# Where the start of a graph kernel gets its small weights: from GpSimd's queue early, or from SyncE's queue behind the large inputs

## The chip, the cores and the metric

The kernel runs on one core of one Trainium2 chip. Times are device microseconds of one execution; the profile is of one profiled execution of the same kernel. The engines are TensorE (PE in the profile, with PEld for its weight loads), VectorE (DVE), ScalarE (ACT), GpSimd (POOL) and SyncE (SP), which only issues transfers here. Transfers can be issued by SyncE, ScalarE and GpSimd.

## The reference

Two layers over 16 batches of 1024 nodes with 64 features, each with a residual and a layer norm. Cut to what is computed:

```python
# layer 0
Q = einsum('bnc,oc->bno', x, Wq) + bq
K = einsum('bnc,oc->bno', x, Wk) + bk
V = einsum('bnc,oc->bno', x, Wv)
score = softmax(einsum('bnc,bmc->bnm', Q, K), axis=1)
score = einsum('bnm,mc->bnc', score, adj)
x = layernorm(x + einsum('bnm,bmc->bnc', score, V))
# layer 1: both supports are adj
x1 = adj @ x
x2 = 2 * adj @ x1 - x
x_cat = concat([x, x1, x2, x1, x2], axis=-1)
x = layernorm(x + x_cat @ weight + bias)
```

The kernel holds the batches in eight pairs, so that a pair has 128 features. It forms adj times x first (the "first product", into a tile U), by a scheme with seven quarter products (p1 to p7) in place of eight, for which VectorE forms sums of quarters of adj and of x. The scores need only one combined weight of Wq and Wk. Of layer 1's five weight blocks three combined ones are left, made on VectorE and stored in the tile `raw`, with Wv and the bias in its last two rows; all five have the mean over their outputs taken away.

## The kernel before

The loads, in the order of the program:

```python
still = const.tile([P, P], FP, ...); nc.vector.memset(still, 0.0)
ident = const.tile([P, P], FP, ...); make_identity(nc, ident)
wq, wk = pair_weight("wq"), pair_weight("wk")        # cleared 128x128 tiles
halves = [slice(j * C, (j + 1) * C) for j in range(2)]   # C = 64
for s in halves:
    nc.scalar.dma_start(wq[s, s], wqT)
    nc.gpsimd.dma_start(wk[s, s], wkT)
for s in halves:
    nc.scalar.dma_start(bkp[s], bk[:, None])
for k in range(0, K8, 4):                             # pair 0 in two halves
    nc.sync.dma_start(xs[:, 0, k : k + 4], x_in[:, 0, k : k + 4])
for p in range(1, NP):                                # pairs 1 to 7
    nc.sync.dma_start(xs[:, p], x_in[:, p])
for k in (4, 5, 6, 7, 0, 1, 2, 3):                    # adj
    nc.sync.dma_start(aT[:, k], a_in[:, k])
for s in halves:
    nc.gpsimd.dma_start(w1s[s], w1.rearrange("(s c) o -> c s o", c=C))
    nc.gpsimd.dma_start(raw[s, 3], wvT)
nc.gpsimd.dma_start(raw[:, 4], b1[None, :].to_broadcast([P, C]))
```

The first work of TensorE. Idle turns multiply a tile of zeros and keep TensorE busy while it would wait:

```python
def transposed(p):
    pt = ps_tile("pt")
    for k in range(K8):
        nc.tensor.transpose(pt[:, ts(k, P)], xs[:, p, k, :], ident)
    nc.scalar.activation(xT[:, p], pt, AF.Copy)

def score_weight():          # transposes Wq and Wk
    ...
def score_weight_2(pm):      # their product, and the product with bk
    ...
def project(p):              # GY[p] = combined weight times xT[p], on TensorE and VectorE
    ...

idle_turns(6)
transposed(0)
idle_turns(3)
transposed(1)
pm = score_weight()
idle_turns(2)
transposed(2)
score_weight_2(pm)
for p in range(NP):
    if p + 3 < NP:
        transposed(p + 3)
    project(p)
```

Then the preparation of the weights, twelve instructions of VectorE, and the first product:

```python
w24 = const.tile([P, C], FP, tag="w24", name="w24")
nc.vector.tensor_add(w24, w1s[:, 2], w1s[:, 4])
...                                                   # combine, then take the means away
wv = pair_weight("wv")
for j in range(2):
    s = slice(j * C, (j + 1) * C)
    nc.vector.tensor_copy(wv[s, s], raw[s, 3])
...
S = left_tiles()
for n in (1, 2, 4, 3):
    left_sum(S, n)                                    # sums of quarters of adj, VectorE
step, sums = product(S, xs, by_pair(U), acc_group=1)
sums(1)                                               # sum of quarters of x, VectorE
for p in range(NP):
    nc.vector.tensor_reduce(mu[:, p], rows_of(p), AX.X, ALU.add)
...
for name in ("p2", "p1", "p5"):
    step(name, 0)
    step(name, 1)
```

The attention loop follows, with the layer norm and layer 1's weights (`wv` and `raw` are first used there), and then two more products with adj.

Of the kernel before, what the change touches and what calls it, by code (L numbers as in the profile page):

```python
# [9 lines left out]
FP = mybir.dt.float32  # L10
AF = mybir.ActivationFunctionType
ALU = mybir.AluOpType
AX = mybir.AxisListType
# [5 lines left out]
def gnn_kernel(  # L19
# [13 lines left out]
    nc = tc.nc  # L33
    ctx.enter_context(tc.manual_schedule())
    N, B, C = out.shape
    P = 128
# [8 lines left out]
    const = ctx.enter_context(tc.tile_pool(name="const", bufs=1))  # L45
# [14 lines left out]
    def pair_weight(name):  # L60
        w = const.tile([P, P], FP, tag=name, name=name)
        nc.vector.memset(w, 0.0)
        return w
# [3 lines left out]
    ident = const.tile([P, P], FP, tag="ident", name="ident")  # L67
    make_identity(nc, ident)
    wq, wk = pair_weight("wq"), pair_weight("wk")
    bkp = const.tile([P, 1], FP, tag="bkp", name="bkp")  # L70
    raw = const.tile([P, 5, C], FP, tag="raw", name="raw")
    w1s = const.tile([P, 5, C], FP, tag="w1s", name="w1s")
    halves = [slice(j * C, (j + 1) * C) for j in range(2)]
    for s in halves:
        nc.scalar.dma_start(wq[s, s], wqT)
        nc.gpsimd.dma_start(wk[s, s], wkT)
    for s in halves:
        nc.scalar.dma_start(bkp[s], bk[:, None])
    for k in range(0, K8, 4):
        nc.sync.dma_start(xs[:, 0, k : k + 4], x_in[:, 0, k : k + 4])  # L80
    for p in range(1, NP):
        nc.sync.dma_start(xs[:, p], x_in[:, p])
    for k in (4, 5, 6, 7, 0, 1, 2, 3):
        nc.sync.dma_start(aT[:, k], a_in[:, k])
    for s in halves:
        nc.gpsimd.dma_start(w1s[s], w1.rearrange("(s c) o -> c s o", c=C))
        nc.gpsimd.dma_start(raw[s, 3], wvT)
    nc.gpsimd.dma_start(raw[:, 4], b1[None, :].to_broadcast([P, C]))

    expo = const.tile([P, G], FP, tag="expo", name="expo")  # L90
    nc.vector.memset(expo, -0.5)
# [12 lines left out]
# [6 lines that stand above are left out]
# [14 lines left out]
    def rows_of(p):  # L124
        return xs[:, p].rearrange("p k (b c) -> p (k b) c", b=2)
# [7 lines left out]
    def idle_turns(n):  # L133

        pt = pacc.tile([P, N], FP, tag="acc", name="idle")
        for _ in range(n):
            nc.tensor.matmul(pt[:, 0:P], still, still, start=True, stop=True)

    idle_turns(6)
    transposed(0)  # L140
    idle_turns(3)
    transposed(1)
    pm = score_weight()
    idle_turns(2)
# [2 lines left out]
    for p in range(NP):  # L147
# [6 lines left out]

    w24 = const.tile([P, C], FP, tag="w24", name="w24")
    nc.vector.tensor_add(w24, w1s[:, 2], w1s[:, 4])
    nc.vector.tensor_sub(raw[:, 0], w1s[:, 0], w24)
    nc.vector.tensor_add(raw[:, 0], raw[:, 0], ident[:, 0:C])  # L160
    nc.vector.tensor_add(raw[:, 0], raw[:, 0], ident[:, C:P])
    nc.vector.tensor_add(raw[:, 1], w1s[:, 1], w1s[:, 3])
    nc.vector.tensor_scalar(raw[:, 2], w24, 2.0, None, op0=ALU.mult)
    rsum = const.tile([P, 5], FP, tag="rsum", name="rsum")
    nc.vector.tensor_reduce(rsum, raw, AX.X, ALU.add)
    nc.vector.scalar_tensor_tensor(
        raw, rsum[:, :, None].to_broadcast([P, 5, C]), -1.0 / C, raw, op0=ALU.mult, op1=ALU.add
    )
    wv = pair_weight("wv")
    for j in range(2):  # L170
        s = slice(j * C, (j + 1) * C)
        nc.vector.tensor_copy(wv[s, s], raw[s, 3])

    def row_sums(sq, g=G):
        var = small.tile([P, g], FP, tag="var", name="var")
# [45 lines left out]
    def by_pair(t):  # L221

        return t.rearrange("p k (q f) -> p q k f", q=NP)
# [189 lines left out]
        left_sum(S, n)  # L413
    step, sums = product(S, xs, by_pair(U), acc_group=1)
    sums(1)
    for p in range(NP):
        nc.vector.tensor_reduce(mu[:, p], rows_of(p), AX.X, ALU.add)
    nc.vector.tensor_scalar(mu, mu, 1.0 / C, None, op0=ALU.mult)
# [179 lines left out]
```

## Time and profile before

| what | value |
|---|---|
| time, median of 3 runs | 620.51 us (619.64 to 621.8) |
| span of the profiled execution | 619.1 us |
| VectorE, ScalarE, GpSimd busy | 54%, 36%, 13% of the span |
| transfers in all | 14.30 MB, 23 GB/s over the span |
| loads of x, adj at the start | 512 KB for each of 8 pairs of x, 8 of 512 KB for adj |

The span in 40 slices of 15.5 us shows TensorE and the transfers (a digit is the busy share in tenths; the first slice is the start that the change edits):

```profile
PE   7999999999999999999999999999999999999995
...
DMA  7700000200000000000000000000000000010012
```

The small transfers, from the page's list of issues (destination, source, issuing queue, count, KB of each, us from issue to landing):

```profile
w1s<-in_w_dram POOLq DMA_DIRECT2D x2, 80.0 KB, 9.1
wq<-in_wqT_dram ACTq DMA_DIRECT2D x2, 16.0 KB, 4.9
wk<-in_wkT_dram POOLq DMA_DIRECT2D x2, 16.0 KB, 6.0
```

A "wait" of an engine in the profile is idle time, put down to the event that ended it. The clock column of the stage views is the share of full speed that TensorE was granted.

### The profile page before, as it was taken

The numbers are of one execution on the slowest core, as the hardware profiler recorded it, in microseconds if no ns is written. First come the engines' busy times: TensorE is split into PE (matmuls) and PEld (weight loads), VectorE is DVE, ScalarE is ACT, GpSimd is POOL, SyncE is SP. The second block draws the span as 40 slices with busy tenths as digits, with TensorE's granted clock in tenths as the row PEclk, the third lists the DMA queues.
The fourth block names the chain that finished last, engine by engine and source line by source line (L and its number), as shares of the span: only waits on it lengthen the run. The fifth ranks groups of instructions, "written<-read, shape, count | busy, mean of one in ns | idle before, by whom it ended". The sixth has DMA issues, their size and how long they took to land. (4 is left out here: it accounts for less than half of the span.)

```text
span 619.1 us, 5817 instructions
## 1 busy us (share of the span) xinstructions
PE 606.8 (98%) x2268; PEld 265.7 (43%) x2268; DVE 337.2 (54%) x560; ACT 225.9 (36%) x379; POOL 82.7 (13%) x47
## 2 busy tenths in 40 slices
PE   7999999999999999999999999999999999999995
PEld 6544444433334344343434434344544444444442
DVE  0598202157786867768686776735462333224544
ACT  3210100056666667676666767651100000000011
POOL 3000004400030300303030020300000000150372
PEclk8999999999999999999999999999999999999999
DMA  7700000200000000000000000000000000010012
GB/s 267 295 0 1 0 1 0 69 0 0 2 1 0 2 0 2 1 0 2 1 0 2 0 2 1 0 1 0 1 0 0 1 0 0 1 68 0 34 69 102
DMA packets 5883, 14.30 MB, mean 23 GB/s; under 512 B 976, under 2 KB 1072, under 8 KB 5856
## 3 DMA queue, kind: packets, MB, share of 16 engines
q1 hardware_dynamic: 5280, 13.63, 5.9%
q8 instruction: 18, 0.29, 0.2%
q0 software_dynamic: 256, 0.26, 0.1%
q10 hardware_dynamic: 320, 0.03, 0.0%
q14 instruction: 9, 0.07, 0.0%
HBM read 9.73 MB, written 4.19 MB: 22 GB/s over the span
## 5 line engine op out<-in xcount | busy, mean ns | idle before, releaser
L327 DVE TENSOR_SCALAR_CACHE_REDUCE e<-sc 128x1024 f32<-128x1024 f32 x128 | 151.6, 1222 | 68.1 <-PE sc L320 68.1
L334 ACT ACTIVATE e<-e,nm 128x1024 f32<-128x1024 f32 x128 | 146.2, 1143 | 74.7 <-DVE e L327 74.6
L320 PE MATMUL sc<-xT,GY 64*128 64x512 f32 x512 | 128.1, 615 | 0.5 <-DVE e L327 0.5
L357 PE MATMUL acc<-e,us 128*64 128x512 f32 x512 | 124.0, 605 | 0.3 <-DVE us L345 0.3
L182 POOL TENSOR_TENSOR rstd<-var,expo 128x16 f32<-128x16 f32 x13 | 37.7, 2902 | 421.5 <-DVE var L177 421.5
L320 PEld LDWEIGHTS sc<-xT,GY 64*128 64x128 f32 x512 | 44.6, 186 | 73.5 <-issue 49.9
L521 ACT ACTIVATE sq<-GY 128x1024 f32<-128x1024 f32 (+1 forms) x10 | 8.9, 886 | 159.6 <-DVE GY L297 149.9
L281 PE MATMUL p<-T,S 128*128 128x512 f32 x144 | 62.8, 592 | 0.0
L357 PEld LDWEIGHTS acc<-e,us 128*64 128x64 f32 x512 | 31.0, 136 | 71.0 <-issue 62.9
L281 PEld LDWEIGHTS p<-T,S 128*128 128x128 f32 x144 | 27.4, 190 | 34.4 <-issue 34.4
L299 ACT ACTIVATE U<-p 128x1024 f32<-128x1024 f32 x6 | 6.1, 1023 | 76.3 <-PE p L281 76.3
L393 PEld LDWEIGHTS pw<-raw,xT 64*128 64x128 f32 x256 | 21.8, 187 | 17.3 <-issue 7.3
L440 POOL TENSOR_TENSOR xs<-xs,mu 128x1024 f32<-128x1024 f32 x8 | 15.0, 1902 | 100.9 <-DVE T L250 90.1
L393 PE MATMUL pw<-raw,xT 64*128 64x192 f32 x256 | 27.1, 332 | 0.0
L404 DVE TENSOR_TENSOR xT<-pw,raw 128x256 f32<-128x256 f32 x32 | 13.6, 425 | 21.3 <-ACT GY L403 21.3
L334 ACT ACTIVATION_READ_ACCUMULATOR e<-e,nm 128x1 f32 x128 | 24.0, 188 | 0.0
L109 ACT ACTIVATE xT<-pt 128x1024 f32<-128x1024 f32 x16 | 16.2, 1013 | 20.0 <-PE pt L108 20.0
L108 PE MATMUL pt<-ident,xs 128*128 128x128 f32 x128 | 18.7, 294 | 3.0 <-DMA xs<-in_x_dram 3.0
L281 PE MATMUL acc<-T,aT 128*128 128x512 f32 x48 | 21.4, 594 | 0.0
L281 PE MATMUL p<-GY,aT 128*128 128x512 f32 x48 | 21.3, 596 | 0.0
L281 PE MATMUL p<-T,aT 128*128 128x512 f32 x48 | 21.3, 592 | 0.0
L281 PE MATMUL acc<-T,S 128*128 128x512 f32 x48 | 21.1, 592 | 0.0
(120 smaller groups left out, 594.5 us busy)
## 6 DMA issues: line engine op xcount, KB each, us to landing
aT<-in_adjT_dram SPq DMA_DIRECT2D x8, 512.0 KB, 10.1
out_dram<-GY SPq DMA_DIRECT2D x16, 256.0 KB, 2.2
xs<-in_x_dram SPq DMA_DIRECT2D x7, 512.0 KB, 9.0
aT<-in_adjT_dram SPq DMA_DIRECT2D x1, 1024.0 KB, 5.0
xs<-in_x_dram SPq DMA_DIRECT2D x2, 256.0 KB, 3.0
w1s<-in_w_dram POOLq DMA_DIRECT2D x2, 80.0 KB, 9.1
wq<-in_wqT_dram ACTq DMA_DIRECT2D x2, 16.0 KB, 4.9
wk<-in_wkT_dram POOLq DMA_DIRECT2D x2, 16.0 KB, 6.0
```

Of the source, the lines that this page charges most:

```text
L108: nc.tensor.transpose(pt[:, ts(k, P)], xs[:, p, k, :], ident)
L109: nc.scalar.activation(xT[:, p], pt, AF.Copy)
L182: nc.gpsimd.tensor_tensor(rstd, var, expo[:, 0:g], ALU.pow)
L281: nc.tensor.matmul(pt[:, ts(i, H)], left_of(k, 2 * g + i), right_of(k), start=(start and k == 0), stop=(k == HB - 1), skip_group_check=not ...
L320: nc.tensor.matmul(sc[j][:, ts(h, H)], GY[s, p, ts(m, P)], xT[s, p, ts(h, H)], start=True, stop=True,)
L327: nc.vector.tensor_scalar(E[n][:, j], sc[j], -1.0, None, op0=ALU.mult, op1=ALU.min, accum_out=NM[n][:, j : j + 1],)
L334: nc.scalar.activation(E[n][:, j], E[n][:, j], AF.Exp, bias=NM[n][:, j : j + 1], scale=-1.0, accum_out=SM[n][:, j : j + 1],)
L357: nc.tensor.matmul(ACC[p][j * C : (j + 1) * C, ts(h, H)], us[:, j], es[:, j, ts(h, H)], start=(m == 0), stop=(m == K8 - 1),)
L393: nc.tensor.matmul(pw[:, j, ts(k, 3 * C)], xT[s, p, ts(2 * c + k, P)], raw[s, 0:3].rearrange("p w c -> p (w c)"), start=True, stop=True,)
L404: nc.vector.tensor_tensor(at(xT), to[:, 0], raw[:, 4:5, None].to_broadcast([P, 2, 2, C]), ALU.add)
L440: nc.gpsimd.tensor_tensor(rows_of(p), rows_of(p), mu[:, p, :, None].to_broadcast([P, G, C]), ALU.subtract)
L521: nc.scalar.activation(sq, r, AF.Square)
```

## The change

Seven transfers leave GpSimd's queue. Wk goes to SyncE's queue, behind the first pair of x and ahead of the second. The second layer's weights, Wv and the bias go to the end of SyncE's queue, behind adj. Since these land later, their preparation on VectorE moves behind the first sums of adj and x. One idle turn is added between the first two pairs. The aim is that the small transfers should not stand in the way of x at the start. No arithmetic changes.

```diff
     for s in halves:
         nc.scalar.dma_start(wq[s, s], wqT)
-        nc.gpsimd.dma_start(wk[s, s], wkT)
     for s in halves:
         nc.scalar.dma_start(bkp[s], bk[:, None])
     for k in range(0, K8, 4):
         nc.sync.dma_start(xs[:, 0, k : k + 4], x_in[:, 0, k : k + 4])
+    for s in halves:
+        nc.sync.dma_start(wk[s, s], wkT)
     for p in range(1, NP):
         nc.sync.dma_start(xs[:, p], x_in[:, p])
     for k in (4, 5, 6, 7, 0, 1, 2, 3):
         nc.sync.dma_start(aT[:, k], a_in[:, k])
     for s in halves:
-        nc.gpsimd.dma_start(w1s[s], w1.rearrange("(s c) o -> c s o", c=C))
-        nc.gpsimd.dma_start(raw[s, 3], wvT)
-    nc.gpsimd.dma_start(raw[:, 4], b1[None, :].to_broadcast([P, C]))
+        nc.sync.dma_start(w1s[s], w1.rearrange("(s c) o -> c s o", c=C))
+        nc.sync.dma_start(raw[s, 3], wvT)
+    nc.sync.dma_start(raw[:, 4], b1[None, :].to_broadcast([P, C]))
 ...
     idle_turns(6)
     transposed(0)
-    idle_turns(3)
+    idle_turns(4)
     transposed(1)
 ...
-    w24 = const.tile([P, C], FP, tag="w24", name="w24")
-    nc.vector.tensor_add(w24, w1s[:, 2], w1s[:, 4])
-    ...                                   (the twelve instructions, unchanged)
+    def layer_weights():
+        w24 = const.tile([P, C], FP, tag="w24", name="w24")
+        nc.vector.tensor_add(w24, w1s[:, 2], w1s[:, 4])
+        ...
+        return wv
 ...
     step, sums = product(S, xs, by_pair(U), acc_group=1)
     sums(1)
+    wv = layer_weights()
     for p in range(NP):
         nc.vector.tensor_reduce(mu[:, p], rows_of(p), AX.X, ALU.add)
```

More of the change, by code (lines that the diff above doesn't have):

```diff
@@ L150, in gnn_kernel @@
         project(p)
-    w24 = const.tile([P, C], FP, tag="w24", name="w24")
-    nc.vector.tensor_add(w24, w1s[:, 2], w1s[:, 4])
[L159 to L172, printed above, removed]
+    def layer_weights():
+        w24 = const.tile([P, C], FP, tag="w24", name="w24")
+        nc.vector.tensor_add(w24, w1s[:, 2], w1s[:, 4])
+        nc.vector.tensor_sub(raw[:, 0], w1s[:, 0], w24)
+        nc.vector.tensor_add(raw[:, 0], raw[:, 0], ident[:, 0:C])
+        nc.vector.tensor_add(raw[:, 0], raw[:, 0], ident[:, C:P])
+        nc.vector.tensor_add(raw[:, 1], w1s[:, 1], w1s[:, 3])
+        nc.vector.tensor_scalar(raw[:, 2], w24, 2.0, None, op0=ALU.mult)
+        rsum = const.tile([P, 5], FP, tag="rsum", name="rsum")
+        nc.vector.tensor_reduce(rsum, raw, AX.X, ALU.add)
+        nc.vector.scalar_tensor_tensor(
+            raw, rsum[:, :, None].to_broadcast([P, 5, C]), -1.0 / C, raw, op0=ALU.mult, op1=ALU.add
+        )
+        wv = pair_weight("wv")
+        for j in range(2):
+            s = slice(j * C, (j + 1) * C)
+            nc.vector.tensor_copy(wv[s, s], raw[s, 3])
+        return wv
     def row_sums(sq, g=G):
```

## The prediction

> **What bounds the kernel now.** I read the busy line of the page first, then stages cut at the places where TensorE (PE) changes its work, then PE's list of waits, then the start in order of time.
>
> The busy line and the stages (start:end, length, then busy time and instruction count of each engine, the granted PE clock, the DMA share and GB/s):
>
> ```profile
> PE 606.8 (98%) x2268; PEld 265.7 (43%) x2268; DVE 337.2 (54%) x560; ACT 225.9 (36%) x379; POOL 82.7 (13%) x47
> ...
> 1.05:6.25 5.20, 5.20 (x26) 4.99 (x26) 0.26 (x4) 1.92 (x2) 4.56 (x8) 1.00 0.74 239
> 6.25:9.28 3.03, 0.00 (x0) 0.00 (x1) 0.00 (x0) 0.39 (x1) 0.00 (x0) 0.91 0.64 222
> 9.28:12.25 2.97, 2.97 (x14) 2.97 (x15) 0.43 (x1) 0.96 (x1) 0.00 (x0) 0.52 1.02 316
> 12.25:31.20 18.95, 18.95 (x85) 11.35 (x84) 9.14 (x9) 6.20 (x7) 0.00 (x0) 1.00 0.78 309
> 31.20:100.00 68.80, 68.80 (x162) 30.52 (x161) 34.92 (x33) 6.14 (x6) 3.98 (x3) 1.00 0.00 0
> 100.00:406.00 306.00, 305.53 (x1442) 122.96 (x1440) 205.48 (x427) 188.25 (x325) 44.60 (x20) 1.00 0.01 4
> 406.00:598.00 192.00, 191.75 (x517) 87.19 (x514) 75.48 (x69) 17.26 (x31) 22.12 (x10) 1.00 0.03 11
> ```
>
> The reader is to see that PE sets the time. From 12.25 us to 598 us it is idle for 0.47 + 0.25 = 0.72 us in all, so whatever happens before 12.25 us shifts everything after it, one for one. Before that point lies one hole of 3.03 us with no PE work, and behind it 2.97 us of work at a clock of 0.52. Those two rows are all that this change can reach on PE. PE's waits, and the PE rows around the hole (start, duration, work, and in brackets the idle time before it and its cause):
>
> ```profile
> PE pt L108 <- DMA xs<-in_x_dram: 3.0, 1, 3.0
> PE idle L137 <- DVE still L66: 1.1, 1, 1.1
> PE sc L320 <- DVE e L327: 0.5, 1, 0.5
> PE acc L357 <- DVE us L345: 0.3, 1, 0.3
> ```
>
> ```profile
> 5.42 0.83 PE L137 MATMUL idle<-still 128*128 128x128 f32 x6
> 9.28 1.97 PE L108 MATMUL pt<-ident,xs 128*128 128x128 f32 x8 [3.03 <-DMA xs<-in_x_dram]
> ...
> 12.25 1.04 PE L108 MATMUL pt<-ident,xs 128*128 128x128 f32 x8
> ```
>
> The hole is the wait for the second pair of x, xs[1]. The same eight transposes take 1.97 us after it and 1.04 us one pair later.
>
> Why is xs[1] late? Its transfer is issued at 1.65 us and takes 7.6 us to land (the DMA view of that issue alone). Sizes and times to landing of undisturbed transfers stand on the page:
>
> ```profile
> xs<-in_x_dram SPq DMA_DIRECT2D x2, 256.0 KB, 3.0
> aT<-in_adjT_dram SPq DMA_DIRECT2D x1, 1024.0 KB, 5.0
> ```
>
> Between them lie 768 KB in 2.0 us, so 512 KB should land in about 3.7 us, half of what it took. In the hole the DMA engines are only 0.64 busy at 222 GB/s: the bandwidth is not used up, something in the mix is slow. The mix is xs on SyncE's queue, Wq and bk on ScalarE's, and seven transfers issued by GpSimd between 1.59 and 5.9 us (Wk twice, the weights twice, Wv twice, the bias). SyncE's own waits show one thing more:
>
> ```profile
> SPq L84 <- DMA xs<-in_x_dram: 3.9, 5, 0.9
> SPq L84 <- DMA bkp<-in_bk_dram: 1.9, 1, 1.9
> SPq L82 <- DMA xs<-in_x_dram: 1.0, 1, 1.0
> SPq L82 <- DMA wq<-in_wqT_dram: 0.5, 1, 0.5
> SPq L82 <- DMA bkp<-in_bk_dram: 0.4, 1, 0.4
> ```
>
> A load of x has no use for Wq or bk, yet it waits for them. After four SyncE and four ScalarE transfers, each further one waits for the landing of an older one. The ninth (xs[3]) was issued at 3.62 us, just when the first half of pair 0 had landed (issued at 0.74, 2.9 us to landing). I read this as eight completion places, shared by the two hardware queues.
>
> **What the Trainium skill says.** (1) "TensorE: Matmul & The Clock Gate", Part 1: The HAM clock gate: a PE idle for a window of about 3.4 us falls to half clock, for at least one window. This trace agrees: 0.52 in the stage behind the hole, and 1.00 from 12.25 us on. (2) "DMA: Bandwidth & Descriptors", Issuing engines are not separate DMA queues: transfers of all issuers share the same 16 engines and interleave, so Wk by SyncE saves no bandwidth; it can only change the order and the way descriptors are made. The trace agrees as far as it goes: during GpSimd's issues xs[1] takes twice its fitted time. (3) The same page, Latency and other measured facts: two of the sixteen DMA engines (7 and 15) are usually slower than the rest, as a best guess because the descriptor rings of GpSimd-issued transfers lie in SBUF behind their ports; transfers issued by SyncE or ScalarE have no such ring. No view here names the DMA engines; a transfer that ends late while the engines are 0.64 busy would fit.
>
> **The change part by part.**
>
> Removed from the start: all seven GpSimd transfers. They carry 2 x 16 + 2 x 80 + 2 x 16 + 32 = 256 KB, half the size of xs[1]. GpSimd's 4.3 us of issue go too, which nobody waited for.
>
> Added ahead of xs[1]: two Wk issues on SyncE, at about 0.45 to 0.6 us each (0.43 for an x issue; 0.6 estimated from ScalarE's two Wq issues in 1.19 us), and 32 KB in the queue, under 0.1 us at 370 GB/s, perhaps twice that since the rows have 256 bytes. SyncE would then be ready to issue xs[1] at about 2.6 to 2.8 us instead of 1.65. But the order is now four ScalarE transfers, pair 0 in two halves, Wk twice: eight. So xs[1] should be the ninth and wait for the first half of pair 0, at 3.64 us. With 3.7 us of flight it lands at about 7.3 us, 2.0 us sooner than the 9.28 of now.
>
> Idle turns, three to four: three turns are six records in 0.83 us, so the fourth costs 0.28 us. The turns then end at 6.25 + 0.28 = 6.53 us, still ahead of 7.3, so this costs nothing. The hole shrinks from 3.03 us to about 0.75 us.
>
> The clock: it was full until about 8.74 us (0.74 in the half microsecond from 8.5) and half for about 3.4 us then. In the 3.4 us before the drop PE worked 0.9 us. With the change it works about 1.2 us before the short hole and 1.4 us after it in the same stretch. I expect it to stay at 1.00. Then pair 1's work runs warm: eight transposes 1.04 us, two weight transposes at 0.13 each 0.27, two idle turns 4 x 0.138 = 0.55, together 1.86 instead of 2.97: 1.11 us less.
>
> Sum: the transposes of pair 2 start at 7.3 + 1.86 = 9.16 us, against 12.25: 3.1 us earlier.
>
> Does what follows keep up? xs[2] is issued when Wq's first half has landed (4.4 us now) and follows xs[1] in the queue by 512 KB at about 400 GB/s (the rate of 14 to 26 us), 1.3 us: 8.6 us, ahead of 9.16. xs[3] by 9.9, wanted at about 10.3. From there a pair costs PE 2.59 us (16.12 to 18.71 in the start's order of time), against 1.3 us for its transfer, so the queue gains. bk is wanted at about 10.3 us; now its second half lands at 3.0 + 9.3 = 12.3 us, in the same crowd that slows xs[1]; without the crowd I expect it by 9. This is the closest margin. adj has wide slack: first used at 31.2 now, landed by 28.6.
>
> Layer weights on VectorE: the twelve instructions run from 33.04 to 35.99 us, 2.95 us. They move behind the first five sums of 2.29 us each. The sums start 2.95 us sooner relative to PE, but PE waits for none of them now (after the very first clearing of a tile, the list has 0.8 us of VectorE waits, both in the attention loop), and the first product that needs one, p5, starts at 59.1. The reductions of x and the first add into U come behind the same total of VectorE work as before. Worth 0. The weights land behind adj, by about 27 us, and VectorE wants them at about 41 us: no wait. Five more SyncE issues end long before SyncE's next job.
>
> **The rivals.** (a) xs[1] lands as late as now, because the slow part is bk's four-byte rows on ScalarE's queue or the load itself: for it, SyncE also waits 1.9 us for bk; against it, that bk too is slowed in the same crowd. Then there is hardly a gain: 620 to 620.5. (b) The ninth place is not where I put it and xs[1] goes out at 2.7 us: landing at 6.4, no hole at all, pair 2 at 6.53 + 1.86 = 8.39, 3.9 us gained: 616.6. (c) The wait moves to bk or xs[3]: PE stops at 10.3 us for up to 2 us: 618 to 619.5. (d) The hole shrinks but the clock still drops: 1.1 us of the gain lost, about 618.5. (e) VectorE work becomes late for the products: would cost up to 3 us, but VectorE is 54% busy and the total ahead of each consumer is unchanged, so I give it little.
>
> **Range and chances.** 620.5 - 3.1 = 617.4. The three times before spread over 2.2 us, from 619.64 to 621.8. With about two thirds on (b) or the main line (616.6 to 617.8), a fifth on (c) and (d), the rest on (a), the range is 616.0 to 619.8. The whole stretch that can be won is 3.03 + 1.11 = 4.1 us, 0.7%, so 2% faster cannot be reached; 2% slower needs a wait of 12 us that nothing here shows.
>
> **What would show it.** Right: PE's wait for xs under 1 us; a clock of 1.00 from the first transposes on; pair 2's transposes at 8.4 to 9.5 us; xs[1] issued near 3.6 us with 3.5 to 4 us of flight; everything after 12.25 us the same, about 3 us earlier. Wrong: a new PE wait at the bk product or at a later pair; the clock at 0.5 somewhere in 8 to 13 us; xs[1] landing after 8 us; a VectorE wait on PE in the first product stage.

## The result, and the profile after

| | before | after |
|---|---|---|
| median of 6 runs | 621.32 us (619.64 to 623.32) | 617.92 us (617.77 to 618.05) |
| ratio | 1 | 0.9945, 95% interval 0.9926 to 0.9964 |
| span of the profiled execution | 619.1 us | 616.0 us |
| first matmul of the first product | 31.64 us | 28.93 us |

The change saves 3.4 us by the medians, 2.2 to 4.6 us by the interval; 617.92 lies in the predicted range. The changed kernel is also steadier: its six runs lie within 0.3 us, those of the kernel before within 3.7 us.

The stages of the kernel after, cut at the same places as in the prediction (start:end, length, busy time and count of PE, PEld, DVE, ACT, POOL, granted PE clock, DMA share, GB/s):

```profile
1.05:6.25 5.20, 5.20 (x28) 5.12 (x28) 0.26 (x4) 1.98 (x2) 0.25 (x1) 1.00 0.64 188
6.25:9.28 3.03, 1.50 (x14) 1.34 (x13) 0.00 (x0) 0.53 (x2) 0.00 (x0) 1.00 1.02 368
9.28:12.25 2.97, 2.97 (x26) 2.73 (x26) 0.78 (x3) 2.21 (x3) 0.00 (x0) 1.00 1.02 417
12.25:31.20 18.95, 18.95 (x70) 10.14 (x69) 11.05 (x9) 4.76 (x5) 0.00 (x0) 1.00 0.76 283
```

PE's waits and its start in order of time, after:

```profile
PE pt L109 <- DMA xs<-in_x_dram: 1.5, 1, 1.5
PE idle L138 <- DVE still L66: 1.1, 1, 1.1
PE sc L323 <- DVE e L330: 0.5, 1, 0.5
PE acc L360 <- DVE us L348: 0.3, 1, 0.3
```

```profile
5.36 1.06 PE L138 MATMUL idle<-still 128*128 128x128 f32 x8
7.95 1.10 PE L109 MATMUL pt<-ident,xs 128*128 128x128 f32 x8 [1.53 <-DMA xs<-in_x_dram]
...
9.54 1.04 PE L109 MATMUL pt<-ident,xs 128*128 128x128 f32 x8
...
10.78 1.07 PE L109 MATMUL pt<-ident,xs 128*128 128x128 f32 x8
...
28.93 11.32 PE L284 MATMUL p<-xs,aT 128*128 128x512 f32 x26
```

The reader is to see three things. The hole in front of pair 1 is 1.53 us instead of 3.03. The clock no longer falls: it is 1.00 from 6.25 us on. (The column has 1.00 in the first stage too, before and after, but the start of that stage is slow in both: the eight transposes of pair 0 take 1.80 us before and 1.75 us after, those of pair 2 1.04 us in both.) And between 6.25 and 9.28 us the transfers move 368 GB/s instead of 222. From pair 3's transposes (10.78 us, 13.49 before) on, PE's work is that of before, 2.71 us earlier: I compared the matmuls of each tile in the two traces at their first, middle and last, and the shift is 2.71 to 2.72 us up to the last one, 611 us into the span. The other 0.4 us between the two spans lie behind the last matmul, in the end of the output.

### The profile page after: what moved, and what is told of

Its sections match the earlier page's. It is cut to its first block, busy times and chain, and to the rows that moved or that the text cites. A ratio compares the mean times of both kernels' runs of the same rounds, so it can differ in the third digit from the quotient of the medians.

```text
span 616.0 us, 5816 instructions
## 1 busy us (share of the span) xinstructions
PE 605.6 (98%) x2270; PEld 264.4 (43%) x2270; DVE 337.1 (55%) x560; ACT 226.0 (37%) x379; POOL 78.4 (13%) x40
## 5 line engine op out<-in xcount | busy, mean ns | idle before, releaser
L284 PE MATMUL p<-S,aT 128*128 128x512 f32 x48 | 21.1, 592 | 0.0
```

Of the source, the lines that this page charges most:

```text
L284: nc.tensor.matmul(pt[:, ts(i, H)], left_of(k, 2 * g + i), right_of(k), start=(start and k == 0), stop=(k == HB - 1), skip_group_check=not ...
```

## The experiments

The figures of the start are from one profiled execution of each kernel, in us from the span's start, so some tenths between two rows may be chance: the four rows of the changed order (after, after_again, prep_first, three_turns) have xs[3] at 10.44 to 10.91. The medians come from several chips; the ratios further down compare with the kernel before on the same chip. "Lands" is the last of a transfer's completions in the trace. Up to sixteen DMA engines work on one transfer and each reports its share (the Trainium skill, "DMA: Bandwidth & Descriptors", Why a DMA increments its semaphore by 16 and not by 1; the traces have sixteen completions for each of these loads). The last column but one is the start of pair 3's transposes.

| kernel | xs[1] issued | xs[1] lands | xs[3] lands | pair 3 | median, us |
|---|---|---|---|---|---|
| before | 1.65 | 9.24 | 13.35 | 13.49 | 620.3 to 621.3 |
| wk_only | 3.49 | 7.84 | 13.09 | 13.23 | 620.70 |
| bridge | 1.66 | 6.66 | 12.62 | 12.76 | 620.31 |
| rest_late | 1.64 | 8.82 | 11.77 | 11.91 | 618.87 |
| rest_late_bk | 1.65 | 8.47 | 11.40 | 11.53 | 619.01 |
| after | 3.65 | 7.90 | 10.44 | 10.78 | 617.92 |
| after_again | 3.62 | 7.45 | 10.88 | 11.01 | 618.13 |
| prep_first | 3.53 | 7.88 | 10.48 | 10.76 | 618.08 |
| three_turns | 3.70 | 7.42 | 10.91 | 11.05 | 618.09 |
| wk_behind_x1 | 1.64 | 6.63 | 11.12 | 11.25 | 618.51 |
| x1_first | 1.63 | 6.31 | 10.83 | 10.96 | 618.08 |
| bk_behind_x2 | 2.84 | 6.91 | 11.51 | 11.64 | 618.98 |
| pair0_whole | 2.70 | 8.13 | 12.06 | 12.20 | 619.19 |
| x_first | 1.65 | 8.87 | 11.32 | 12.27 | 620.02 |

In all but three rows (after, prep_first and x_first) pair 3 starts 0.13 to 0.14 us after xs[3] has landed, and in all but x_first, which has another order of work, the first product starts 18.14 to 18.15 us after pair 3. xs[1] explains the product's start nowhere nearly so well: it lands between 6.3 and 9.2 us with little relation to it.

### Each half of the change alone

wk_only: Wk on SyncE behind pair 0; the other loads stay on GpSimd, the preparation stays in its old place, three turns.

```diff
     for s in halves:
         nc.scalar.dma_start(wq[s, s], wqT)
-        nc.gpsimd.dma_start(wk[s, s], wkT)
 ...
+    for s in halves:
+        nc.sync.dma_start(wk[s, s], wkT)
     for p in range(1, NP):
```

> The kernel before with Wk alone moved to SyncE behind pair 0; the layer-1 weights, Wv and the bias stay on GpSimd at the start, three idle turns. Theory (the crowd of GpSimd transfers slows xs[1], and the ninth transfer waits for pair 0's first half): xs[1] goes out near 3.65 us, meets the weights in flight, lands no earlier than 9 us, and nothing is gained: 620 to 622.5, a clock of 0.5 behind the hole. Rival (Wk's place is what brings the gain): xs[1] lands by 8 us and the time is 618 to 619.

Measured: ratio 1.000 (0.9989 to 1.001). The time is what the theory said, the reason is not: xs[1] landed at 7.84 us, as the rival had it. PE in order of time, wk_only:

```profile
7.88 1.10 PE L109 MATMUL pt<-ident,xs 128*128 128x128 f32 x8 [0.98 <-DMA xs<-in_x_dram]
...
11.92 1.06 PE L109 MATMUL pt<-ident,xs 128*128 128x128 f32 x8 [2.28 <-DMA xs<-in_x_dram]
```

The wait for pair 1 shrank and one of 2.28 us for pair 2 stood in its place; pair 3 then started 0.26 us sooner than before. So curing the hole that the profile of before shows is worth nothing by itself: xs[3] landed at 13.09 us, hardly sooner than the 13.35 of before.

rest_late: only the weights, Wv and the bias move behind adj; Wk stays on GpSimd, the preparation in place.

```diff
-        nc.gpsimd.dma_start(w1s[s], w1.rearrange("(s c) o -> c s o", c=C))
-        nc.gpsimd.dma_start(raw[s, 3], wvT)
-    nc.gpsimd.dma_start(raw[:, 4], b1[None, :].to_broadcast([P, C]))
+        nc.sync.dma_start(w1s[s], w1.rearrange("(s c) o -> c s o", c=C))
+        nc.sync.dma_start(raw[s, 3], wvT)
+    nc.sync.dma_start(raw[:, 4], b1[None, :].to_broadcast([P, C]))
```

> The kernel before with only the weights, Wv and the bias moved behind adj on SyncE; Wk stays on GpSimd, the preparation stays where it was, three idle turns. Theory: five GpSimd transfers fewer, and xs[1] still goes out at 1.65 us with no ninth place in its way, so it lands at 5.5 to 7.5 us, as early as or earlier than in the changed kernel (7.9 us); the clock stays at 1.00; 616.5 to 618. Rival (any GpSimd transfer in front slows it, or Wk's move was needed): xs[1] lands after 8.5 us, 619 to 621.

Measured: ratio 0.9978 (0.9967 to 0.9989). xs[1] landed at 8.82 us, hardly sooner than before, so the theory's landing (5.5 to 7.5) failed, and yet the first product came 1.59 us earlier, because xs[3] landed at 11.77 instead of 13.35. PE in order of time, rest_late:

```profile
8.87 1.10 PE L108 MATMUL pt<-ident,xs 128*128 128x128 f32 x8 [1.89 <-DMA xs<-in_x_dram]
...
11.91 1.06 PE L108 MATMUL pt<-ident,xs 128*128 128x128 f32 x8
```

The two halves together (0.27 and 1.59) are less than the whole (2.71 us). The medians on one chip say the same: 620.58 before, 620.70 wk_only, 618.87 rest_late, 618.08 with the changed order (prep_first).

What rest_late does not tell apart: its five transfers both leave GpSimd's queue and move their 224 KB behind x. No run issued them late from GpSimd, or early from SyncE. By an estimate from the traces (later pairs of x, 512 KB each, land 1.28 us apart) 224 KB take 0.56 us, so the bytes alone would not account for the 1.58 us by which xs[3] came sooner.

### The clock, the place of the preparation, the fourth turn

bridge: `idle_turns(3)` becomes `idle_turns(13)` in the kernel before.

> The kernel before with 13 idle turns instead of 3 between the first two pairs (ten more, 2.8 us), nothing else. Theory: xs[1] still lands at about 9.3 us, but PE works through the wait, the clock stays at 1.00, and only the slow part is won: pair 2 starts at about 11.1 instead of 12.25 us, 1.1 us less, 619.3 to 620.3. Rival (the clock falls by its own schedule and not by the hole): no gain.

Measured: ratio 0.9997 (0.9984 to 1.0009), no gain in the median to be told from noise: neither the theory's gain nor the rival's falling clock. Only the highest times are gone: its 12 runs reach at most 621.09 us, and 11 of the 43 runs of the kernel before beside it lie above that. In its profile the clock did hold, and pair 2 started at 10.78 us instead of 12.25. But xs[3] came at 12.62 us:

```profile
9.24 1.04 PE L108 MATMUL pt<-ident,xs 128*128 128x128 f32 x8
...
10.78 1.04 PE L108 MATMUL pt<-ident,xs 128*128 128x128 f32 x8
...
12.76 1.06 PE L108 MATMUL pt<-ident,xs 128*128 128x128 f32 x8 [0.59 <-DMA xs<-in_x_dram]
```

xs[1] here landed at 6.66 us, in the same order of loads as before: the order alone does not fix when it lands.

prep_first: `wv = layer_weights()` goes back in front of `S = left_tiles()` in the changed kernel.

> The changed kernel with the twelve instructions for the weights put back in front of the sums of adj. Theory (their place is worth 0, as PE never waits for VectorE there): 617.7 to 618.1, the same as the changed kernel, the first product at the same 28.9 us. Rival: the sums come late for the product p5 and PE waits up to 3 us: 619 to 621.

Measured: 618.08 us, ratio 0.9963 (0.9951 to 0.9976); the first product at 28.91 us. The place of the preparation is worth nothing that shows.

three_turns and after_again: the changed kernel with `idle_turns(3)`, and the changed kernel itself beside it.

> The changed kernel with three idle turns as before the change. Theory (the fourth turn lies in the wait for xs[1] and the clock holds without it): PE's wait for xs[1] 0.1 to 0.3 us longer, the first product at the same 28.9 us, 617.8 to 618.1 with the same narrow spread. Rival (the fourth turn is what keeps the clock up): some runs 1 us longer, median 618.3 to 619.

> The changed kernel once more, beside the other two on the same chip: 617.7 to 618.2, the first product at 28.7 to 29.1 us.

Measured: 618.09 us (617.52 to 618.35), ratio 0.9947 (0.9927 to 0.9967), and 618.13 us (617.78 to 619.14), ratio 0.9945 (0.992 to 0.9969). The fourth turn is worth nothing here. Both profiles had a second short wait, for xs[3] (0.61 and 0.48 us), and so the first product at 29.19 and 29.16 us, a little later than expected.

### Is it GpSimd's queue that slows xs[1], and can the start be shortened further?

Four kernels with Wk on SyncE or GpSimd, and bk on ScalarE or behind xs[2]. wk_behind_x1, x1_first and bk_behind_x2 start from the changed kernel, rest_late_bk from rest_late:

```diff
     for p in range(1, NP):
         nc.sync.dma_start(xs[:, p], x_in[:, p])
+        for s in halves:
+            if p == 1:                               # wk_behind_x1, x1_first
+                nc.sync.dma_start(wk[s, s], wkT)
+            elif p == 2:                             # x1_first, bk_behind_x2, rest_late_bk
+                nc.sync.dma_start(bkp[s], bk[:, None])
```

(each with the old load of the same tensor taken out)

> The changed kernel with Wk behind the second pair of x instead of ahead of it. xs[1] is then among the first eight transfers and goes out at 1.65 us, as in rest_late, and no GpSimd transfer is left. Theory A (GpSimd-issued transfers are what slows xs[1]): it lands 4.2 us later, near 6 us; PE's wait for it is gone, Wk lands by 8 us; the first product starts near 28 us, 616.8 to 617.5. Theory B (small rows on ScalarE's queue, Wq and bk, beside a large load slow it in the same way): it lands after 8 us as in rest_late (8.9), the first product at 29 us or later, 618 to 619.

> The same with bk also moved to SyncE, behind xs[2]: only Wq is on ScalarE's queue. Theory A: as wk_behind_x1, near 6 us, 616.8 to 617.5, unless bk now comes late for its product at 9.5 us. Theory B: xs[1] now lands by 6.5 us, about 2 us sooner than in wk_behind_x1, and the time is about 1 us lower than there.

> The changed kernel with bk moved to SyncE behind xs[2], Wk still ahead of xs[1]. xs[1] becomes the seventh transfer and goes out at 2.8 us instead of 3.65. Theory (the ninth place costs what it looks like): it lands about 0.8 us sooner, near 7.1 us, and the first product starts 0.8 us sooner, near 28.1: 617.0 to 617.4. Rival (the stop for the ninth place is what lets the small rows through; xs[1] then flies as much longer as it leaves sooner): 617.7 to 618.5.

> rest_late (Wk on GpSimd, xs[1] out at 1.64 us) with bk moved to SyncE behind xs[2]. Theory A: the two GpSimd transfers of Wk still slow xs[1], which lands after 8 us, 618.5 to 619.3. Theory B: with bk out of the way xs[1] lands near 6.5 us; Wk then sets pair 2: 617 to 618.

Measured: ratios 0.9974 (0.9961 to 0.9987), 0.9953 (0.9937 to 0.9968), 0.9973 (0.9959 to 0.9986) and 0.9969 (0.9959 to 0.998). xs[1] landed at 6.63 and 6.31 us without GpSimd's Wk and at 8.82 (rest_late) and 8.47 us with it, whether bk was there or not. These four agree with theory A and not with B (x_first below will overturn A). But the gain did not come. x1_first has the earliest xs[1] of all, with no wait for it left, and its waits moved to bk and to a later pair:

```profile
PE pt L110 <- DMA xs<-in_x_dram: 0.9, 1, 0.9
PE sc L324 <- DVE e L331: 0.5, 1, 0.5
PE pw L122 <- DMA bkp<-in_bk_dram: 0.4, 1, 0.4
```

Pair 3 started at 10.96 us, no sooner than in the changed kernel. In bk_behind_x2 xs[1] came 1.0 us sooner than in the changed kernel and the first product 0.86 us later.

pair0_whole: pair 0 in one transfer, so that xs[1] is the eighth.

```diff
-    for k in range(0, K8, 4):
-        nc.sync.dma_start(xs[:, 0, k : k + 4], x_in[:, 0, k : k + 4])
+    nc.sync.dma_start(xs[:, 0], x_in[:, 0])
```

> The changed kernel with pair 0 loaded by one transfer of 512 KB instead of two halves, so that xs[1] is the eighth transfer and no longer waits for a place. Theory (the ninth place holds xs[1] back, and with all small rows still ahead of xs[2] nothing else comes late): xs[1] goes out near 2.6 us, lands near 7 us instead of 7.9, and the first product starts up to 0.9 us sooner than the changed kernel's 28.9: 617.0 to 617.5. Rival (the wait moves to a later pair or bk, as in bk_behind_x2): the first product at 28.9 or later, 617.8 to 619.

Measured: 619.19 us, ratio 0.997 (0.9958 to 0.9982), 1.1 us slower than the changed kernel on the same chip (after_again), and slower than the rival had it. xs[1] left 0.95 us sooner than in the changed kernel, as foreseen, flew 5.4 us instead of 4.3, and xs[3] landed at 12.06.

x_first: no small load at all in front of pairs 0 to 3; the order of TensorE's work changed to suit.

```diff
+        if p == 3:        # behind xs[3]
+            ...           # Wq, Wk and bk, all on SyncE
     transposed(1)
-    pm = score_weight()
-    idle_turns(2)
     transposed(2)
-    score_weight_2(pm)
+    transposed(3)
+    pm = score_weight()
+    idle_turns(2)
+    score_weight_2(pm)
     for p in range(NP):
-        if p + 3 < NP:
-            transposed(p + 3)
         project(p)
+        if p + 4 < NP:
+            transposed(p + 4)
```

> The changed kernel with pairs 0 to 3 of x first and alone, and Wq, Wk and bk behind them on the same queue; TensorE transposes pairs 0 to 3, then makes the score weight, then projects. Theory (what bounds the start is how soon the first pairs of x come, and every small row in their way costs it): xs[1] lands by 6.0, xs[3] by 8.5 us, TensorE waits for the score weight's parts instead, which land by 10 us; the first product at 27.6 to 28.3 us instead of 28.9 to 29.2, 616.5 to 617.4. Rival (the bound then is the small rows themselves, which come in behind 2 MB of x): they land after 10.5 us, the first product at 29 us or later, 618 us or more.

Measured: 620.02 us, ratio 0.9991 (0.9977 to 1.0004): the theory failed. With no small load ahead of it, and none from GpSimd at all, xs[1] needed nearly as long as in the kernel before (7.2 and 7.6 us). The small rows landed at 11.5 to 12.6 us, as the rival had it, and the first product came at 32.44. The DMA view of xs[1]'s issue, PE in order of time, and the stage from 9 to 12 us, x_first:

```profile
xs<-in_x_dram SPq DMA_DIRECT2D x1, 512.0 KB, 7.2
```

```profile
8.91 4.40 PE L109 MATMUL pt<-ident,xs 128*128 128x128 f32 x24 [2.44 <-DMA xs<-in_x_dram]
13.14 0.27 PE L114 MATMUL pw<-ident,wq 128*128 128x128 f32 x1
```

```profile
9.00:12.00 3.00, 3.00 (x15) 3.00 (x16) 0.00 (x0) 1.02 (x1) 0.00 (x0) 0.50 0.38 78
```

In this profile the clock also fell to 0.50, which drew out the transposes. That is not all that keeps x_first from a gain: in 15 of its 20 runs the granted clock averaged 0.996 or more over the run, a sign that it did not fall (this profile has 0.995), and their median is still 619.7 us.

So GpSimd's transfers are not needed for xs[1] to be late. The completions of xs[1]'s sixteen shares show the form of it (us, from the traces):

```
                12th of 16    16th
before             6.17       9.24
rest_late          6.43       8.82
x_first            5.97       8.87
bridge             6.04       6.66
wk_only            7.45       7.84
x1_first           5.91       6.31
after              7.11       7.90
```

In the kernels with a late xs[1] twelve shares land by 6.0 to 6.4 us and the last 2.4 to 3.1 us behind them. Few shares hang so far behind: in x_first fourteen are down by 6.03 us and two land at 8.80 and 8.87, in rest_late likewise two (8.71 and 8.82); in the kernel before and in rest_late_bk only the last does (9.24 after 7.44, 8.47 after 6.08). The lag lasts: in x_first fourteen shares of xs[3] are down by 9.66 us, the last two at 11.25 and 11.32. The long lag was seen in four of the five kernels that issue pairs 0, 1 and 2 back to back (before, rest_late, rest_late_bk, x_first, not bridge), and in none of those with Wk's rows between pairs 0 and 1 or 1 and 2, where the last was 0.2 to 0.8 us behind (in pair0_whole the lag began earlier: eight were done at 6.39 us, twelve at 7.91, all at 8.13). Why a few shares hang behind, and whether a mere pause would cure it as Wk's rows do, was not tried and stays open.

## Why the prediction was right, point by point

**What bounds the start: half seen.** That everything behind the start only shifts was right, to 0.01 us over 580 us of matmuls. But I took the wait on xs[1] for the bound because it is the only one that the profile of before names, and read the missing idle time behind 12.25 us as a sign that nothing else binds. xs[3] stood right behind it: PE began pair 3 0.14 us after xs[3] had landed (13.35 us), which shows as no wait because PE was late enough itself:

```profile
13.49 1.07 PE L108 MATMUL pt<-ident,xs 128*128 128x128 f32 x8
```

The DMA views of xs[3]'s issue (3.62 us before, 4.83 us after; the last figure is the time to landing):

```profile
xs<-in_x_dram SPq DMA_DIRECT2D x1, 512.0 KB, 9.7
```

```profile
xs<-in_x_dram SPq DMA_DIRECT2D x1, 512.0 KB, 5.6
```

Issued 1.21 us later, it lands 2.9 us sooner. Of the 2.9 us, 1.6 are the earlier landing of its twelfth share (11.55 us before, 9.92 after) and 1.3 the shorter lag of the last share behind that one (1.80 before, 0.52 after). That is the gain in the trace; the wk_only and bridge kernels show that without it the shorter hole and the held clock bring nothing to the median.

**xs[1] as the ninth transfer: right.** It went out at 3.65 us as worked out, from the place that pair 0's first half had freed. Its flight of 3.7 us was mis-sized: 4.3 us here, 3.7 to 4.4 us in the four profiles of this order. The landing at 7.3 was 7.9.

**The hole and the clock: right in kind.** The hole came out at 1.5 us, not 0.75; the clock stayed at 1.00 and the work of pair 1 took 1.6 us (7.95 to 9.54) instead of 2.97; 1.86 was reckoned, by adding durations that overlap in the trace (eight transposes of 1.04 us, and the next row starts 0.87 us after their start). Pair 2 began at 9.54 instead of 9.16. So three of the prediction's own signs of being right were narrowly missed: a wait under 1 us (1.53), pair 2 by 9.5 us (9.54), a flight of at most 4 us (4.25).

The prediction says that this trace agrees with its rule for the clock, an idle window. That is too strong: the clock fell at about 8.74 us, when PE had idled for 2.5 us, and the length of the hole does not decide by itself. In x_first a hole of 2.44 us went with a fall, in rest_late_bk one of 2.79 us did not.

The fall is also not in every execution of the kernel before. In 65 of its 133 runs beside the experiments the granted clock averaged 0.990 to 0.995 over the run (the profiled one, with the fall, has 0.995), in the other 68 it averaged 0.996 to 0.998; the medians are 621.7 and 620.0 us. All 12 runs of the changed kernel have 0.996 to 0.998, and about 618.0 us. So against runs of the kernel before in which the clock seems to have held the change wins about 2 us, and its steadiness goes with a clock that never fell. Whether the fall itself or late loads that come with it cost the 1.7 us between the two groups is not told apart: bridge, with a clock of 0.996 to 0.998 in all its 12 runs, has a median of 620.3.

**Does what follows keep up: the step that was too light.** "xs[3] by 9.9, wanted at about 10.3" came out at 10.44, wanted at 10.78: just enough, and in two of the other three profiles of this order 0.5 to 0.6 us late. In the same paragraph it should have been asked when xs[3] landed before. At 13.35 us it would have eaten the gain, had it not moved too. The prediction did ask where xs[3] lands after the change, so its sum is not mere luck; that the margin was enough in this profile (0.34 us) is. The sum of 3.1 us (2.7 in the trace, 3.4 by the medians of the first comparison, 2.6 beside after_again) came near because the same change that freed xs[1] freed xs[3].

**GpSimd's crowd: in part right for xs[3], not for xs[1].** With all seven GpSimd transfers or five of them at the start, xs[3] lands at 12.6 to 13.4 us; with only Wk's two at 11.4 to 11.8; with none at 10.4 to 10.9 in the order of the change, but at 10.8 to 12.1 in other orders. So those five at the start go with a late xs[3] in every kernel; for Wk's two the place of the other small loads counts as much. For xs[1], x_first shows a flight of 7.2 us with no GpSimd transfer at all. So the guess that the Trainium skill offers for slow DMA engines ("DMA: Bandwidth & Descriptors", Latency and other measured facts: descriptor rings of GpSimd-issued transfers) does not cover x_first, where two of sixteen shares hang behind without such transfers. The page names two usually slow engines; the traces do not say which engines these shares belong to. That moving five transfers away from GpSimd and from the start helps xs[3] is shown (rest_late); by what means is not.

**VectorE's part and the fourth turn: worth 0,** as said (prep_first, three_turns).

**The rivals.** (c), the wait that moves on to bk or xs[3], was met by the change only in two of its four profiles, with 0.5 to 0.6 us, but it is what met every attempt to go further: wk_behind_x1, x1_first, bk_behind_x2 and pair0_whole. None has a better median than the changed kernel; x1_first is level with it.

## What to carry to other kernels

A wait at the head of a stream of loads hides the next ones: before mending it, set each later load's landing beside the time its consumer would want it after the mend. A load that lands exactly when its consumer happens to be ready is a bound, though no view calls it a wait. Order the small loads by what they hold up, and measure the order: here "small ones between pair 0 and pair 1" was 2 us better than "last" (x_first), and against "later" (wk_behind_x1, 616.9 to 621.5 us) above all steadier; a sooner issue of xs[1] alone won nothing.

## What the runs showed that I had not expected

- The same 512 KB load, issued at 1.65 us between pairs 0 and 2 without a break, took 5.0 us in one profile and 6.8 to 7.6 in four others, with one or two of the sixteen shares far behind. The kernel before spread over 618.8 to 624.6 us in all its runs, the changed kernel over 617.8 to 619.1.
- A later issue can land sooner: xs[1] issued at 3.49 to 3.70 us landed at 7.4 to 7.9, issued at 1.64 to 1.66 us at 8.5 to 9.2 in four of the five kernels with the pairs back to back.
- Small rows can be dear in the middle of a stream: in bk_behind_x2 half a kilobyte of bk behind xs[2] went with a landing of xs[3] at 11.5 us, 3.3 us after xs[2] (8.22); in x1_first, with the same place of bk, the two are 3.2 us apart, in rest_late_bk 1.7; in the changed kernel they are 1.3 us apart (9.12 and 10.44).
